# Second-level products of halves in the last projection of a cross-attention block

## The chip, the core and the metric

The program runs on one core of a Trainium2 chip. The core has TensorE (in the profile PE for its matmuls and PEld for its weight loads), VectorE (DVE), ScalarE (ACT), GpSimd (POOL) and SyncE (SP, here only a queue that issues transfers), all working side by side from their own instruction streams and waiting for one another through semaphores. Matmul results land in PSUM, eight banks of 128 x 512 float32; everything else lies in SBUF, and the large arrays in HBM. The metric is the device time of one execution in microseconds (us); smaller is better.

## The reference

Everything is float32. B = 4 batches, 512 rows of x and 512 rows of context each, D = 512, 16 heads of 32, inner width 2048.

```
x = layer_norm(hidden, ln1_w, ln1_b)
q = (x @ q_w + q_b); k = (enc @ k_w + k_b); v = (enc @ v_w + v_b)       # 16 heads of 32
attn = softmax(where(mask, q k^T / sqrt(32), min))
out = (attn v) @ cproj_w + cproj_b
hidden = out + hidden
y = layer_norm(hidden, ln2_w, ln2_b)
y = gelu(y @ fc_w + fc_b)          # "fc":   512 -> 2048
y = y @ proj_w + proj_b            # "Proj": 2048 -> 512
return hidden + y
```

## The kernel before

The whole program is one list of steps, the string ORDER. Each token names a step and its indices; the same token again carries on with that step's next part. The program emits instructions in just that order, so the string fixes the order on every engine and on every queue: an engine that must wait at its next instruction holds up all its later ones.

The front part is attention. For each of 16 groups w (4 batches by 4 groups of 4 heads) and each quarter qt of the queries: `u` makes four heads' scores on TensorE, `x` takes the maximum on VectorE and the exponentials on ScalarE, `r` transposes on VectorE, `e` exchanges blocks between partitions with 16 SBUF-to-SBUF transfers of SP's queue, `a` multiplies by v. Steps `k`, `q`, `v` make the projections, `c` the output projection. Between them lie layer norms (`s`, `r1`, `n`, `t`) and the fc step of the batch that has come through attention.

fc is made in eight chunks c per batch, each of 256 inner columns by 512 rows. A chunk is a 2 x 2 block product done by seven products of halves instead of eight (Strassen's scheme in Winograd's form): sums of weight halves by `fs` (GpSimd, function w_sums), sums of y halves by `y`, seven products in four steps `f`, then joins `j` and the gelu `g`. The result of batches 0 to 2 lies in one of two buffers of the ring `stage` until GpSimd's queue has stored it in the HBM array gd. The last batch's chunks (`lw`, `sw`, `z`, `zj`, `zg`) are made after attention, among the Proj products; there the weight sums are VectorE's, and the result stays in SBUF (`ga`).

Proj is, for each batch, again a 2 x 2 block product by seven products of halves, now of 256 columns by 256 rows by 1024 deep. `lg` loads gd into `ga`, which lies where attention's transposes were (the tile swap). `gs` makes the sums of g on VectorE (function g_sums, at most two of the three results live in the tile mix), `ps` those of the weights (p_sums, into ptt). `P` (function project, line 637 in the profile) makes one product in two halves t of 128 rows, each of 8 accumulating matmuls with a moving operand 256 wide. `J` (project_join) copies or adds the products in PSUM into the tile hids, which already holds the residual and the bias (`hd`, `pb`), and stores the rows. Four of these adds a batch run on GpSimd.

A float32 matmul of the program is two matmul records in the profile: the 448 matmuls of Proj are 896 records. Lines 281 and 284 are the helpers for one addition and one subtraction; line 278 is the helper for a transfer on SP's queue.

## Time and profile before

| what | value |
|---|---|
| median of 3 runs (lowest to highest) | 791.18 us (789.69 to 792.59) |
| profiled execution, its own time | 789.92 us |
| span of that execution, first to last instruction | 788.1 us |
| granted TensorE clock | 1.000 |
| chain that ended last, PE's share | 91% |
| attention's last scores on PE start at | 501.40 us |
| first Proj product on PE starts at | 541.29 us |
| HBM read, written | 65.03 MB, 20.97 MB |

Rows of grouped instructions read: line, engine, operation, written tile <- read tiles, shape, count | busy us, mean ns of one | idle time of the engine before them, and what ended it. Rows in order of time read: start us, length us, engine, line, operation, tiles, shape, count in a run, and in brackets the idle time before the run with its releaser. The mean of one instruction includes its latency; back to back, the next one starts before the former has ended, so rates are taken from starts.

## The change

It does three things.

Each of Proj's products is made by seven products again: its left and right factors are quartered, sums of the quarters of the left factor are made by `xs` (four VectorE operations of 512 elements for each batch and product), those of the right factor by `pt` (four, once per product number), seven sub-products with a moving operand 128 wide and 4 deep replace the two halves of 8, and `pj` joins them into a row buffer (one ScalarE copy and four VectorE adds). Three of the 28 products stay as they were (PLAIN): products 1 and 2 of batch 0 and product 4 of batch 3, which is the last of all.

The first-level sums of g are made by GpSimd as soon as a chunk has its gelu (`gs`, now per chunk: four operations of 256 elements), and stored in gd beside g by a second transfer of GpSimd's queue. gd is kept by left factor: seven blocks a batch, each loaded by one transfer of 1 MB (`la`, 28 in all, into four buffers in turn). The sums have one buffer in SBUF, 384 KB, at the end of the tile mix, where the last thirds of the second `xs` buffer and of the sums ws3 lie too.

The last batch's fc is made like the others': weight sums on GpSimd, result through `stage` and gd. All adds of `J` are VectorE's now, between SBUF operands. The bias row of Proj is loaded late (`lr`), into the place of v's. The whole list ORDER was made anew.

```diff
 ORDER = """
+k:0 k:0 wk:2 qb s1:0 s1:0 s1:0 s1:0 r1:0 n1:0 n1:0 n1:0 n1:0 k:1 t1:0:1 t1:0:1 t1:0:0 t1:0:3 t1:0:2 t1:0:0 t1:0:2 m:0
+  t1:0:3 q:0 q:0
+u:0:0 x:0:0 x:0:0 x:0:0 x:0:0 v:0 r:0:0
...
+  f:3:4 P:0:6 g:3:3 g:3:3 fs:3:5 fs:3:6 fs:3:5 fs:3:5 gs:3:3 gs:3:3 gs:3:3 gs:3:3 gs:3:3 j:3:4 j:3:4 j:3:4 j:3:4
+  fs:3:6 fs:3:5 fs:3:6 pt:6 ps:4 pt:4 pj:0:6 f:3:4 f:3:5 j:3:4 fs:3:6 g:3:4 f:3:5 f:3:5 f:3:6 P:0:5 g:3:4 j:3:5 gs:3:4
...
+  j:3:7 f:3:7 j:3:7 j:3:7 P:0:5 pj:0:6 P:0:5 J:0:1 xs:0:7 xs:0:7 P:0:7 J:0:6 xs:0:7 xs:0:3 pj:0:7 la:0:4 g:3:7 g:3:7
+  gs:3:6 gs:3:6 gs:3:6 gs:3:6 gs:3:6 P:0:3 P:0:7 xs:0:4 xs:0:4 pj:0:5 xs:0:3 xs:0:4 pj:0:5 gs:3:7 gs:3:7 gs:3:7 gs:3:7
+  gs:3:7 P:0:4 P:0:7 P:0:4 la:1:6 xs:0:5 xs:0:3 P:0:3 pj:0:3 pj:0:4 pt:5 pt:4 pj:0:4 pj:0:5 P:0:5 la:1:1 pj:0:7 pj:0:7
...
-    gd = [dram.tile([P, NP, 2, L], F32, tag=f"gd{b}", name=f"gd{b}") for b in range(LAST)]
+    gd = [dram.tile([P, 7, NP, HL], F32, tag=f"gd{b}", name=f"gd{b}") for b in range(B)]
...
+    gs = mix[:, 29 * D // 2 :].rearrange("p (s l) -> p s l", s=3)
+    xs = [mix[:, (9 + 3 * i) * D : (12 + 3 * i) * D].rearrange("p (s c l) -> p s c l", s=3, c=NP // 2) for i in range(2)]
...
+    ga = [swap[:, 2 * (i // 2), i % 2 * 4 * D : (i % 2 + 1) * 4 * D].rearrange("p (c l) -> p c l", c=NP) for i in range(4)]
...
+    ws3 = mix[:, 15 * D :].rearrange("p (c n) -> p c n", c=NP // 2)
...
+    def joins(g, names, key, own):
...
+        nc.scalar.copy(g[:, 1], q(0)[:, 0])
+        done(0)
+        yield
+        add(nc.vector, g[:, 0:4:3], q(1), g[:, 1:2].broadcast_to([P, 2, n]))
+        done(1)
+        yield
+        add(nc.vector, g[:, 1:3], q(2), g[:, 3:4].broadcast_to([P, 2, n]))
+        yield
+        add(nc.vector, g[:, 3], q(2)[:, 0], g[:, 2])
+        done(2)
+        yield
+        add(nc.vector, g[:, 1:3], q(3), g[:, 1:3])
+        done(3)
...
+    def g_sums(b, c):
+        g = S["g", b, c].rearrange("p i (j l) -> p (i j) l", j=2)
+        a11, a21, a12, a22 = (g[:, i] for i in range(4))
+        yield from a_sums(nc.gpsimd, a11, a12, a21, a22, gs[:, 0], gs[:, 1], a21, gs[:, 2])
+        yield
+        nc.gpsimd.dma_start(out=gd[b][:, :4, c], in_=g)
+        stage.done("g", b, c)
+        nc.gpsimd.dma_start(out=gd[b][:, 4:, c], in_=gs)
...
+    def load_g(b, n):
+        load(ga[TURN[b, n] % 4], gd[b][:, AT[n]])
...
+    def p_sums2(n):
+        b, t = p_terms(n)
+        return b_sums(nc.vector, *b, *t)
...
+    def g_sums2(b, n):
+        a, s = g_terms(b, n)
+        return a_sums(nc.vector, *a, *s)
 
     def project(b, n):
...
+        if (b, n) in PLAIN:
...
+        def product(o, x, y):
+            h = NP // 2
+            for c in range(h):
+                nc.tensor.matmul(o, x[:, c], y[:, c], start=(c == 0), stop=(c == h - 1))
...
+        product(bank(2, "p1")[:, 0], a11, b11)
+        yield
+        q = bank(3, "p26")
+        product(q[:, 0], a12, b21)
+        product(q[:, 1], s2, t2)
+        yield
+        q = bank(0, "p57")
+        product(q[:, 1], s3, t3)
+        product(q[:, 0], s1, t1)
+        yield
+        q = bank(1, "p34")
+        product(q[:, 0], s4, b22)
+        product(q[:, 1], a22, t4)
...
     def project_join(b, n):
...
+        def join(i, j, n):
+            o = h[i][:, :, j * HL : (j + 1) * HL]
+            add(nc.vector, o, o, of(n))
...
-        elif n == 7:
-            add(nc.vector, u3p, q, u2p)
-            yield
-            join(nc.gpsimd, 1, 1, u3p)
...
+        elif n == 7:
+            add(nc.vector, S["r", b, n], S["r", b, n], S["r", b, 6])
+            done(6)
+            yield
+            join(1, 1, n)
```

## What was predicted

> **What bounds the kernel now.** I read busy times first, then the waits of TensorE, then stretches of the span.

> ```profile
> PE 778.2 (99%) x4370; PEld 538.2 (68%) x4370; DVE 565.9 (72%) x1145; ACT 361.0 (46%) x764; POOL 188.6 (24%) x230
> ```
> ```profile
> PE acc L470 <- DMA swap<-swap: 3.1, 1, 3.1
> PE acc L708 <- POOL nhalf L697: 1.3, 1, 1.3
> PE sc L419 <- ACT pbt L398: 0.8, 1, 0.8
> PE sc L419 <- DVE mn L427: 0.8, 1, 0.8
> ```
> ```profile
> 500.00:550.00 50.00, 50.00 (x272) 34.49 (x271) 26.05 (x47) 16.39 (x27) 8.74 (x13) 1.00 0.96 313
> 550.00:600.00 50.00, 50.00 (x233) 43.93 (x232) 36.63 (x55) 2.40 (x4) 16.30 (x16) 1.00 0.36 139
> ...
> 750.00:788.10 38.10, 34.94 (x162) 30.40 (x161) 10.24 (x16) 0.00 (x0) 7.08 (x5) 1.00 0.18 59
> ```

> TensorE has matmuls running in 778.2 of 788.1 us; the four waits make 6.0 of the missing 9.9, the end 3.2. Of the stretches (length, then busy us of PE, PEld, DVE, ACT, POOL, clock, DMA share) the first two have no gap on PE at all, at full clock. So the time is the sum of TensorE's streams, and what counts is how long a stream takes and whether the others keep up.

> ```profile
> 541.29 3.62 PE L637 MATMUL acc<-pbt,swap 128*128 128x256 f32 x16
> 544.75 7.07 PE L637 MATMUL sc<-ptt,mix 128*128 128x256 f32 x32
> ...
> 9.51 3.73 PE L406 MATMUL acc<-ptt,ext 128*128 128x128 f32 x32
> 13.09 3.60 PE L384 MATMUL acc<-ext,ptt 128*128 128x512 f32 x8
> ```

> From start to start, 16 records 256 wide take 3.45 us, 0.216 each; 32 records 128 wide (v's projection, a new weight load for each) take 3.58, 0.112 each.

> **TensorE's saving.** A product was 2 x 8 matmuls, 32 records: 32 x 0.216 = 6.91 us. It becomes 7 x 4 matmuls, 56 records of v's very shape: 56 x 0.112 = 6.27. That is 0.64 less, and 25 products of 28 change: **-16.0 us**. The other bound is the mean by group, where run-outs count too:

> ```profile
> L406 PE MATMUL acc<-ptt,ext 128*128 128x128 f32 x512 | 60.8, 277 | 0.0
> ```

> 60.8 / 512 = 0.119 a record, 6.65 a product, -6.4 us in all. I take -16.0, since v's records stand in a closed stream as the new ones will. fc's matmuls are as many as before.

> **The head.** Before the first scores, v:0 (the 32 records above) filled a wait; in the new list it stands behind them.

> ```profile
> 13.60 1.91 DVE L313 TENSOR_SCALAR xn<-xn,mv,rs 128x512 f32<-128x512 f32 x4 [1.45 <-POOL rs L300]
> 16.52 2.16 PE L320 MATMUL acc<-ident,xn 128*128 128x128 f32 x16
> 22.91 1.14 PE L419 MATMUL sc<-pbt 32*128 32x512 f32 x8 [0.78 <-ACT pbt L398]
> ```

> The transposes need normalized rows, ready at 15.5. Without v:0 TensorE is free at 13.1 instead of 16.5, can transpose about 1.0 sooner, and owes 3.58 of work: **+2.6 us**. The wait of 3.1 for an exchange may go: its transfers stand a block earlier in SP's list, ahead of the four context loads that they followed. Between 0 and -3.1, I take **-1.6**.

> **VectorE's new work**, from these rows:

> ```profile
> 686.23 0.69 DVE L284 TENSOR_TENSOR mix<-mix,swap 128x512 f32<-128x512 f32 x1
> 686.83 0.69 DVE L281 TENSOR_TENSOR swap<-sc,swap 128x512 f32<-128x512 f32 x1
> ...
> L281 DVE TENSOR_TENSOR ext<-sc,ext 128x256 f32<-128x256 f32 x8 | 3.4, 421 | 20.2 <-POOL ext L281 13.5 <-PE sc L637 6.7
> ```

> An add of 512 costs 0.60 from start to start, one of 256 0.42 less the same overlap, 0.34. For 128 no row exists; the step from 512 to 256 carried on gives 0.20, and the bounds are 0 and 0.34. I split the new tail in two. **Stretch A**, from the first step of the last batch's fc to batch 1's first product: TensorE has 8 fc chunks of 28 records 256 wide, 48.3, and product steps and a transpose of 32.1, so 80.4 us. VectorE has 51 adds between two SBUF tiles (18 xs, 21 pt, 7 ps, 3 y, 2 J; 30.6), fc's joins (24 of 512, 8 of 256; 17.1) and 4 of the rest: 52. **Stretch B**, from there to the end: TensorE 20 products at 6.27, 3.5 left over from batch 0 and the plain one at 6.9, 135.8; VectorE 82 xs, 41 J, 6 pt (129 x 0.60 = 77.4), pj 67 of 256 and 22 of 128 (27.2), and 0.7: 105. So VectorE is at 65% and 78%, and its price is nothing as long as TensorE's streams cover it; if that cover goes, each us is one.

> GpSimd takes some cover away:

> ```profile
> 574.26 1.76 DVE L284 TENSOR_TENSOR ptt<-pbt,ptt 128x512 f32<-128x512 f32 x1
> 575.94 1.75 DVE L284 TENSOR_TENSOR swap<-swap 128x512 f32<-128x512 f32 x1
> 577.61 1.75 DVE L284 TENSOR_TENSOR ptt<-pbt,ptt 128x512 f32<-128x512 f32 x1
> ...
> 572.80 7.69 POOL L281 TENSOR_TENSOR ext<-ext,row 128x512 f32<-128x512 f32 x5
> ```

> ```profile
> 737.25 1.71 POOL L281 TENSOR_TENSOR ext<-ext,row 128x512 f32<-128x512 f32 x1
> ...
> L281 POOL TENSOR_TENSOR xn<-xn,row 128x512 f32<-128x512 f32 x16 | 20.4, 1274 | 135.4 <-DMA xn<-x_dram 135.3
> ...
> 686.54 2.92 POOL L281 TENSOR_TENSOR ext<-ext,row 128x512 f32<-128x512 f32 x2 [56.67 <-DMA ext<-xa]
> ```

> VectorE adds between SBUF tiles take 1.75 instead of 0.69 while GpSimd adds: 1.07 lost, and GpSimd's own go from 1.27 to 1.71. The add from PSUM of the row 686.83 stays at 0.69, although GpSimd was adding then. Stretch B has 12 bias adds on GpSimd: 12 x 1.07 = 13, so VectorE needs 118 of 135.8. The slack is thin, xs, pj and J share one queue, and a J that waits for a bias holds up the xs behind it. Bounds 0 and +8; I take **+2**.

> [...]

> **GpSimd's chain in stretch A** is the dearest doubt.

> ```profile
> 485.92 0.74 POOL L281 TENSOR_TENSOR wsum<-ext 128x256 f32<-128x256 f32 x1
> 486.74 0.74 POOL L284 TENSOR_TENSOR ext<-ext 128x256 f32<-128x256 f32 x1
> 487.43 0.73 POOL L284 TENSOR_TENSOR wsum<-wsum,ext 128x256 f32<-128x256 f32 x1
> ...
> L578 POOL DMA_DIRECT2D gd<-st x24: 531/571/622, 204.5 to 558.5; - x24
> ...
> DMA to landing us min/median/max: 2.9/5.0/7.5
> ```

> The sums of g have one buffer, so a chunk's first sum waits until the former chunk's store has landed. A cycle is four sums at 0.70, 0.57 for the issue of g, then 5.0 from the issue of the sums to their landing: 8.4 us; the weight sums (fs, 2.8) and bias adds lie inside that wait. From the first chunk's last step to the eighth's TensorE has 41.4 us of fc and 8.1 of product steps between: 7.1 per chunk. So GpSimd falls 1.3 behind per chunk, 9 after seven. Who waits: product 5 of batch 0 needs its last xs sum, which is written where this buffer lies; in TensorE's list 14.4 us of steps stand between the last fc step and that one, and the last joins, gelu, sums and landing take about 1.3 + 1.4 + 2.8 + 5.6 + 0.7 = 11.8. The stall is 9 - 2.6 = 6.4; with landing at 3.5 us there is none. The stores now go in runs of 1 KB (512 pieces instead of 128), which no row shows: an issue costs between 0.57 and, at four times, 2.3. With 2.3 for each of the two, and GpSimd's sums stretched in collisions by 0.45 (1.27 to 1.71), a cycle takes up to 11 and the stall reaches +25. Nearest are the rows of stores of the same kind in a chip less loaded than in attention (DMA share 0.36 against 0.96): I take **+5**, range 0 to +25.

> In attention the sums of 24 chunks bring 24 x 3.4 = 82 us to a GpSimd that is busy for 188.6 in the whole span, most chunks a score block or more from the next; VectorE there works mostly with one SBUF operand, which no row shows disturbed. I take 0. The loads and the end:

> ```profile
> swap<-gd SPq DMA_DIRECT2D x12, 1024.0 KB, 8.1
> ```
> ```profile
> 777.87 7.07 PE L637 MATMUL sc<-ptt,swap 128*128 128x256 f32 x32
> 784.98 0.42 DVE L281 TENSOR_TENSOR ext<-sc,ext 128x256 f32<-128x256 f32 x1 [2.96 <-PE sc L637]
> ```

> The 28 loads of 1 MB, 8.1 us from issue to landing, have four buffers and 6.3 us per product, so three products (19 us) cover one: 0 as well. The last half product, its add and its store keep their form, and the 3.2 us after the last matmul stay.

> **Sum.** 789.9 - 16.0 + 2.6 - 1.6 + 5 + 2 = **781.9 us**. The profiled run's 789.92 is 1.3 below the median of the runs, 791.18; I leave the forecast at 782.

> **Rivals.**
> 1. *All of it is covered.* No stall in A or B, the exchange wait gone: 789.9 - 16.0 + 2.6 - 3.1 = 773.4. For it: VectorE's 65% and 78%. Against: the 8.4 us cycle.
> 2. *GpSimd becomes the bound of the last fc, slower.* Place: the one buffer of sums and the stage ring. It decides once the cycle exceeds 9.9: then lag 7 x 2.8 less 2.6 is 17, all that the rest of the sum (776.9) leaves to 793.6. At 12.2 us (landing at 7.0, collisions 1.8) the stall is 33: 810. For it: landings up to 7.5, four times the pieces. Against: median 5.0 under heavier traffic.
> 3. *VectorE becomes the bound of stretch B.* It decides when a product costs VectorE over 6.8 us; it now costs 105 / 20 + 0.65 = 5.9. If each of the 20 products waits 1 us in its queue, time is 782 + 20 - 2 = 800. For it: 220 adds in one list. Against: no engine of the old tail shows such waits on PE.
> 4. *The narrow streams don't gain what a closed stream gains*, 0.119 a record: 781.9 + 9.6 = 791.5, no change.

> **How the numbers follow.** Chances: forecast (776 to 788) 0.50, rival 1 0.18, rival 2 0.17, rival 3 0.10, rival 4 0.05. Below 772 or above 800 lies most of rival 2's upper half and little else, about 0.15. What a measurement can tell from no change is about 0.3%, 788.8 to 793.6: faster 0.50 + 0.18 + 0.03 of rival 3 = 0.71; slower 0.17 + 0.06 = 0.23; the same 0.06.

> **What would show it.** Rows of `P` 128 wide at 0.112 from start to start and PE busy near 762 confirm the saving. The head is right if PE idles about 2.5 us ahead of the first transposes. [...] It is wrong if PE busy doesn't fall by some 16, or if PE's waits exceed 25 us.

## The result, and the profile after

The changed kernel takes 831.38 us (829.35 to 834.29) where the kernel before, in four runs now, takes 790.45 (789.69 to 792.59): 1.0516 times as long, 95% interval 1.0476 to 1.0556. The forecast was 782, the range ended at 800. The profiled execution took 832.2 us, 50.3 more than the 781.9 of the sum.

The busy times of the page of after, and TensorE's longest waits there (for whom: total us, times, longest):

```profile
PE 779.2 (94%) x4970; PEld 553.4 (67%) x4970; DVE 651.4 (78%) x1290; ACT 371.0 (45%) x791; POOL 326.1 (39%) x414
```
```profile
PE acc L565 <- ACT st L589: 10.7, 6, 5.4
PE acc L565 <- POOL wsum L321: 5.9, 2, 4.5
PE acc L702 <- DVE mix L321: 5.8, 2, 5.2
PE acc L507 <- issue: 4.6, 1, 4.6
PE sc L702 <- DVE st L318: 3.5, 2, 2.7
```

Line 565 is fc's product, 702 the second-level product, 507 the step that multiplies by v; 589 is ScalarE's first copy of a chunk into a stage buffer, 318 and 321 are the helpers for one addition and one subtraction. Span less busy time is 51.2 us. The forecast had 17.9 idle (9.9 + 2.6 - 1.6 + 5 + 2) and 762.2 busy, so 33.3 us are more idle time and 17.0 are matmuls that ran longer.

Stretches of after (length, then busy us of PE, PEld, DVE, ACT, POOL, clock, DMA share, GB/s):

```profile
500.00:550.00 50.00, 43.56 (x252) 29.30 (x250) 31.77 (x62) 25.05 (x44) 34.26 (x48) 1.00 0.82 231
...
600.00:650.00 50.00, 41.35 (x211) 35.44 (x210) 37.72 (x44) 10.19 (x19) 44.66 (x55) 0.93 0.42 145
650.00:700.00 50.00, 41.43 (x314) 40.27 (x313) 34.70 (x63) 2.67 (x7) 11.52 (x14) 0.90 0.49 173
700.00:750.00 50.00, 50.00 (x450) 50.00 (x449) 44.67 (x80) 2.19 (x9) 8.88 (x6) 1.00 0.65 212
```

Before, PE was busy throughout 500 to 600. Now 6 to 9 us are lost in each of the first three stretches shown. In the last fc (600 to 650) GpSimd, 39% busy over the span, is busy for 44.7 of 50 us, and the clock is below 1. Where Proj alone runs (700 to 750) there is no gap, and the narrow products go at the forecast rate, 8 records in 0.89 us:

```profile
705.04 1.06 PE L702 MATMUL acc<-pbt,swap 128*128 128x128 f32 x8
705.94 1.06 PE L702 MATMUL sc<-ptt,mix 128*128 128x128 f32 x8
706.83 1.06 PE L702 MATMUL sc<-mix,swap 128*128 128x128 f32 x8
```

How a wait comes about, from the rows of GpSimd and then of PE at the end of attention (start, length; in brackets the idle time before, and its releaser):

```profile
467.24 0.75 POOL L622 DMA_DIRECT2D gd<-mix  x1
...
475.43 0.72 POOL L318 TENSOR_TENSOR mix<-st 128x256 f32<-128x256 f32 x1 [5.99 <-DMA gd<-mix]
476.23 0.73 POOL L321 TENSOR_TENSOR st<-st 128x256 f32<-128x256 f32 x1
476.92 0.73 POOL L321 TENSOR_TENSOR mix<-mix,st 128x256 f32<-128x256 f32 x1
477.60 0.73 POOL L321 TENSOR_TENSOR wsum<-pbt,wsum 128x256 f32<-128x256 f32 x1
```
```profile
478.38 2.08 PE L565 MATMUL acc<-yT,wsum 128*128 128x256 f32 x4 [4.52 <-POOL wsum L321]
```

The next chunk's first sum waits 5.99 us for the former store to land. A weight sum for another chunk stands three instructions behind it, and TensorE stands still until that is made. At the place that the prediction named, product 5 of batch 0, rows of GpSimd, VectorE and PE in three fences:

```profile
599.67 0.79 POOL L620 DMA_DIRECT2D gd<-st  x1
...
668.45 1.17 POOL L321 TENSOR_TENSOR mix<-mix,st 128x256 f32<-128x256 f32 x1
669.70 1.06 POOL L321 TENSOR_TENSOR mix<-st,mix 128x256 f32<-128x256 f32 x1
670.70 0.79 POOL L620 DMA_DIRECT2D gd<-st  x1
671.49 0.75 POOL L622 DMA_DIRECT2D gd<-mix  x1
```
```profile
676.03 0.69 DVE L321 TENSOR_TENSOR mix<-swap,mix 128x512 f32<-128x512 f32 x1 [5.52 <-issue]
```
```profile
677.50 2.08 PE L702 MATMUL acc<-swap,mix 128*128 128x128 f32 x8 [5.22 <-DVE mix L321]
```

The store of the last batch's first chunk is issued at 599.67 and that of its last at 670.70, seven cycles of 10.1 us. The last sums leave at 671.49, VectorE's sum that is written over them starts at 676.03, and PE waits 5.22. (The last two stores of sums land 3.9 and 4.4 us after their issue starts.) Its 8 records then take 2.08 us instead of 1.06, since the clock fell meanwhile (stretches of 1 us):

```profile
674.00:675.00 1.00, 0.00 (x0) 0.00 (x0) 0.00 (x0) 0.00 (x0) 0.00 (x0) 1.00 1.04 422
...
676.00:677.00 1.00, 0.00 (x0) 0.00 (x0) 0.94 (x2) 0.00 (x0) 0.00 (x0) 0.50 0.00 0
...
681.00:682.00 1.00, 1.00 (x7) 1.00 (x6) 0.04 (x1) 0.00 (x0) 0.00 (x0) 0.50 0.00 0
...
683.00:684.00 1.00, 1.00 (x11) 1.00 (x11) 1.00 (x3) 0.00 (x0) 0.00 (x0) 1.00 0.48 66
```

Some 3.5 us into the gap the granted clock is halved, and it stays so for about 5 us of work: 2.6 us lost on top of the gap. Summed over stretches of 0.5 us, seven gaps of 2.2 to 5.4 us cost 12.9 us of clock in this way, most of the 17.0.

## The experiments

The theories tested first were S (the one buffer of sums), R (the ring of two stage buffers) and Q (GpSimd's work itself). Each table row gives the median of the runs of that kernel, its ratio to the kernel before run beside it with the 95% interval, and, from its one profiled execution: the start of the last batch's first fc step on PE, the time from there to the end of its last fc step, and from there to the end of the last matmul.

| kernel | us | ratio | first fc step | last fc | behind it |
|---|---|---|---|---|---|
| after | 831.38 | 1.0516 (1.0476 to 1.0556) | 579.7 | 73.5 | 173.7 |
| neither sums nor second store | 782.37 | 0.9936 (0.9856 to 1.0016) | 559.3 | 62.0 | 155.8 |
| sums alone | 799.55 | 1.0146 (1.0077 to 1.0216) | 563.6 | 74.0 | 158.5 |
| second store alone | 798.79 | 1.0135 (1.0092 to 1.0178) | 573.6 | 62.1 | 156.1 |
| second store alone, by SP | 793.29 | 1.0042 (1.0004 to 1.0081) | 569.6 | 61.9 | 156.2 |
| sums of 16 columns alone | 783.86 | 0.9932 (0.9899 to 0.9964) | 560.2 | 62.6 | 155.7 |
| those with a fill behind each | 815.11 | 1.0302 (1.0190 to 1.0414) | 580.4 | 70.3 | 160.0 |
| both for batches 0 to 2 | 809.25 | 1.0228 (1.0050 to 1.0405) | 580.8 | 62.5 | 155.9 |
| both for batch 3 | 805.01 | 1.0174 (1.0059 to 1.0290) | 558.5 | 70.2 | 169.3 |
| two buffers of sums | 817.66 | 1.0353 (1.0249 to 1.0457) | 581.6 | 69.2 | 158.9 |
| three stage buffers | 834.33 | 1.0564 (1.0462 to 1.0666) | 585.5 | 73.1 | 167.8 |
| both rings larger | 817.42 | 1.0373 (1.0281 to 1.0465) | 584.4 | 73.6 | 156.8 |
| two buffers, weight sums first | 814.18 | 1.0298 (1.0188 to 1.0408) | 576.5 | 71.0 | 161.4 |
| batch 3's sums on VectorE | 841.54 | 1.0679 (1.0635 to 1.0724) | 583.0 | 80.8 | 172.0 |
| batch 3's weight sums on VectorE | 828.35 | 1.0464 (1.0424 to 1.0504) | 581.8 | 76.5 | 164.7 |
| that with two buffers | 813.41 | 1.0275 (1.0218 to 1.0332) | 574.0 | 75.6 | 157.0 |
| that for batch 2 too | 820.09 | 1.0360 (1.0299 to 1.0420) | 580.2 | 76.7 | 156.4 |
| all products plain | 823.67 | 1.0418 (1.0287 to 1.0549) | 581.4 | 75.8 | 158.8 |

How well such marks repeat: up to the last fc, "both for batch 3" is the kernel with neither, and "both for batches 0 to 2" is after. Their rows of the first step, and those of neither and of after:

```profile
558.51 1.17 PE L565 MATMUL acc<-yT,ext 128*128 128x256 f32 x4
```
```profile
559.28 1.17 PE L565 MATMUL acc<-yT,ext 128*128 128x256 f32 x4
```
```profile
580.76 1.17 PE L565 MATMUL acc<-yT,ext 128*128 128x256 f32 x4
```
```profile
579.70 1.17 PE L565 MATMUL acc<-yT,ext 128*128 128x256 f32 x4
```

These agree within about 1 us. Another pair, two buffers of sums with and without batch 3's weight sums on VectorE, has group 15's first scores at 479.9 and 483.2, ahead of any difference between the two kernels. So differences of the marks below 4 us are not read.

**The rings.**

```diff
-    gs = mix[:, 29 * D // 2 :].rearrange("p (s l) -> p s l", s=3)
+    gs2 = const.tile([P, 3 * HL], F32, tag="gs2", name="gs2")
+    gs_of = [t.rearrange("p (s l) -> p s l", s=3) for t in (mix[:, 29 * D // 2 :], gs2)]
...
-    stage = Ring(const.tile([P, 2 * L], F32, tag=f"st{i}", name=f"st{i}") for i in range(2))
+    stage = Ring(const.tile([P, 2 * L], F32, tag=f"st{i}", name=f"st{i}") for i in range(3))
```

> The changed kernel with two buffers of 3 KB per partition for GpSimd's sums of g, used in turn, instead of one. The room comes from the bias rows: one row serves all three biases, so the biases added are not the reference's; the instructions are the same. Theory S (one buffer of sums: GpSimd stands 33.1 us in 11 waits for gd<-mix to land, its later weight sums stand behind that, and TensorE behind those): these waits go to under 5 us, PE's idle time from 45.7 to about 20, the granted clock rises to about 0.99 and the time falls to 795 to 805. Theory R (the ring of two stage buffers holds ScalarE's first copy of a chunk, 45.1 us in 17 waits): the stage waits stay, 820 to 830. Theory Q (GpSimd has simply too much in its queue next to each chunk): 820 to 830 too.

> The changed kernel with three stage buffers instead of two; the sums keep their one buffer. The room comes from the bias rows as in the run before (one row for all three biases, so the biases are not the reference's) and from fewer buffers for the small tiles of the layer norms. Theory R: ScalarE's waits for gd<-st fall from 45.1 to under 10 us, PE's waits on the copy into st (10.7 + 3.1 us, and what the clock loses after them) go, 800 to 810. Theory S: a chunk still waits at its sums, 820 to 830, with GpSimd's waits for gd<-mix at 30 us or more. Theory Q: 820 to 830.

> The changed kernel with both two buffers for GpSimd's sums and three stage buffers. The room comes from one bias row for all three biases, from t4 of y lying in t1's place and s4 of fc's weights in s1's place, so the biases and two of fc's seven products are not the reference's; the instructions are as many. Theory: once the sums' landing no longer holds GpSimd's queue, the stage ring is what is late next (37.1 us of ScalarE's waits, 10.6 us of PE's with two buffers of sums alone): 796 to 806, PE idle near 22 us. If a third stage buffer is worth nothing here either, as it was alone, 812 to 818.

Two buffers take 14 us off, fewer than theory S gave and more than R and Q did. By the marks they gain 14.8 behind the last fc, where product 5's last sum needn't wait for the last landing any more, 4 in it, and nothing ahead of it: the wait of 5.99 us shown above isn't what attention loses by. A third stage buffer is worth nothing, alone (834, above all bands) or with the second buffer of sums: theory R falls. With both rings larger the stretch from 600 to 650 reads:

```profile
600.00:650.00 50.00, 40.19 (x195) 34.50 (x194) 36.71 (x46) 8.40 (x17) 47.11 (x57) 0.97 0.44 149
```

GpSimd is busy for 47.1 of 50 us. With little left to wait for in this stretch it is close to being a bound itself.

**Sums and store, one by one.** Four kernels make a square: both, either, neither.

```diff
-        yield from a_sums(nc.gpsimd, a11, a12, a21, a22, gs[:, 0], gs[:, 1], a21, gs[:, 2])
+        for _ in range(4):
+            yield
...
-        nc.gpsimd.dma_start(out=gd[b][:, 4:, c], in_=gs)
```

> The changed kernel without GpSimd's four sums per chunk (128 instructions, 102 us of its busy time): both stores stay, the second one stores zeros, so products 3, 5, 6 and 7 of Proj are not the reference's. Theory Q: PE idle falls below 15 us and the time to 780 to 790. Theory S: the landing wait is now one for the issue of the next store alone, most of it gone as well, 790 to 800. Theory R: stores are issued about 3 us sooner, so half of the stage waits go, 805 to 815. If the second-level products or their sums on VectorE are what costs, the time stays above 820.

> The changed kernel without the second store of each chunk: GpSimd still makes the four sums, but nothing of them goes to gd, and products 5, 6 and 3 of Proj load g's own first three blocks instead, 1 MB each as before, so these products are not the reference's. It takes away the landing that the one buffer of sums waits for, 24 us of issues on GpSimd and 12.6 MB of traffic. If the landing is the whole matter, it equals the run with two buffers, 812 to 818; if GpSimd's issues and the traffic count too, 800 to 808; if GpSimd's adding time is what counts, it stays above 818, since the run without sums gave 799.

> The changed kernel with neither GpSimd's sums nor the second store (products 3, 5, 6 and 7 of Proj are not the reference's). What is left of the change is the new order, the second-level products and the last batch's fc made through the stage buffers. If the second-level products give what they were forecast to give, 779 to 785, with PE idle near 14 us. If the second store's traffic and issues don't matter, it equals the run without the sums, 796 to 801; if the second-level products themselves lose, above 790 as well, with waits of PE inside Proj.

Neither: 782.4, where the forecast's sum without its 5 us for GpSimd gives 776.9. Busy times of that kernel, and its stretches of the last fc and of Proj:

```profile
PE 762.5 (98%) x4970; PEld 543.8 (70%) x4970; DVE 637.8 (82%) x1290; ACT 370.8 (48%) x791; POOL 202.9 (26%) x254
```
```profile
600.00:650.00 50.00, 48.88 (x375) 46.85 (x374) 41.96 (x78) 7.34 (x16) 7.89 (x9) 1.00 0.36 124
650.00:700.00 50.00, 50.00 (x450) 50.00 (x450) 46.45 (x85) 2.20 (x9) 9.14 (x6) 1.00 0.70 240
700.00:750.00 50.00, 49.93 (x444) 49.55 (x444) 38.10 (x72) 1.76 (x7) 5.89 (x4) 1.00 0.65 228
```

TensorE is busy for 762.5 us, and Proj runs without gaps. So the second-level products and the loads lose nothing there; the 5 us more are idle time (18.1 of the span against 12.9), short waits in attention. Even this kernel is not told apart from the one before (0.9936, up to 1.0016). The sums alone cost 17 us, the store alone 16, both 49. The marks show where. Ahead of the last fc the store costs 14.3 and the sums 4.3 (both: 20.4). In the last fc the sums cost 12 and the store nothing. Behind it only the two together cost anything, 17.9.

**What of the store costs.** The second store of zeros, from SP's queue:

```diff
-        nc.gpsimd.dma_start(out=gd[b][:, 4:, c], in_=gs)
+        nc.sync.dma_start(out=gd[b][:, 4:, c], in_=gs)
```

> As the run without GpSimd's sums (799 us), but the second store, of zeros, is issued by SP's queue instead of GpSimd's; products 3, 5, 6 and 7 of Proj are not the reference's. The bytes and pieces are the same, and GpSimd is spared 32 issues. Leaving this store out altogether took the time from 799 to 782. If GpSimd's 24 us of issues are what it costs, 782 to 787. If it is the traffic (12.6 MB more among the exchanges of attention), 794 to 801, with PE's waits for the exchanges as they were.

793.3, just under the band given for the traffic: of the 16 us about 5 go with GpSimd's issues and 11 stay, all ahead of the last fc. That these are the bytes is not shown, though, because SP's queue also issues attention's loads, and the stores hold it up. One of TensorE's two longest waits in attention, 3.23 us, is for a load of fc's weights. Rows of SP with neither sums nor store, then of SP and PE with the store by SP:

```profile
464.46 0.91 SPq L315 DMA_DIRECT2D pbt<-fc_w_dram  x2
```
```profile
458.91 1.98 SPq L622 DMA_DIRECT2D gd<-mix  x3
...
467.50 1.01 SPq L315 DMA_DIRECT2D pbt<-fc_w_dram  x2
```
```profile
474.55 2.05 PE L565 MATMUL acc<-yT,pbt 128*128 128x256 f32 x4 [3.23 <-DMA pbt<-fc_w_dram]
```

Three stores take 2.0 us of the queue, the loads behind them are slower to issue, and this one is issued 3.0 us later. Nor are the pieces the same: the stores are 12,800 packets from SP's queue and 3,584 from GpSimd's. So the price of the bytes by themselves stays open; the exchanges' median time to landing, 3.0 us, is the same with neither and with GpSimd's store alone.

**What of the sums costs.**

```diff
+        a11, a12, a21, a22, s1, s2, s4 = (a[:, :16] for a in (a11, a12, a21, a22, *(gs[:, i] for i in range(3))))
...
+            nc.gpsimd.memset(mix[:, 29 * D // 2 : 29 * D // 2 + 720], 0.0)
```

(The second added line, once behind each of the four sums, is that of the run with the fill.)

> As the run without the second store (799.6 us), but each of GpSimd's sums covers 16 columns instead of 256: as many instructions at the same places with the same waits, a small part of the adding time. Products 3, 5, 6 and 7 of Proj are not the reference's. If the 17 us that the sums cost there come from the time they take on GpSimd (0.76 to 0.86 each) and from VectorE's loss beside them, 782 to 788. If they come from the place of the waits (a sum that waits for the gelu holds the weight sums behind it), 794 to 801.

> As the run with sums of 16 columns and no second store (783.9 us), with a fill of 720 columns of the sums' buffer on GpSimd behind each of the short sums, so that GpSimd is about as long at work as with the full sums but writes only and reads nothing. Products 3, 5, 6 and 7 of Proj are not the reference's. If the 17 us of the full sums (799.6 us) are GpSimd's own time in its queue, 795 to 802. If they are what VectorE and GpSimd take from one another when both work on SBUF (VectorE was busy 652.5 us with the full sums, 636.3 with the short ones), 782 to 788 and VectorE's busy time stays near 637, unless a fill disturbs it as an add does.

The short sums cost 1.5 us, so the place of the waits costs nothing by itself. Busy times with full sums, with short ones, and with short ones and the fill:

```profile
PE 767.6 (96%) x4970; PEld 545.3 (68%) x4970; DVE 652.5 (82%) x1290; ACT 370.6 (46%) x791; POOL 300.6 (38%) x382
```
```profile
PE 764.9 (98%) x4970; PEld 544.3 (70%) x4970; DVE 636.3 (81%) x1290; ACT 370.6 (47%) x791; POOL 232.7 (30%) x382
```
```profile
PE 772.9 (95%) x4970; PEld 547.1 (67%) x4970; DVE 637.5 (78%) x1290; ACT 370.9 (46%) x791; POOL 321.3 (39%) x510
```

With the fill GpSimd is busy 21 us longer than with the full sums, VectorE is undisturbed (637.5), and the time is 815, worse than the band. GpSimd's time alone is enough to do harm. The 16 us that VectorE loses beside full sums (652.5 against 636.3) aren't needed for it; that they cost nothing isn't shown. In the last fc the fill costs 8 us where the full sums cost 12, but ahead of it 21 where they cost 4, so it does not stand for the sums there; why stays open.

**Attention and the last fc.**

```diff
-        nc.gpsimd.dma_start(out=gd[b][:, 4:, c], in_=gs)
+        if b < LAST:
+            nc.gpsimd.dma_start(out=gd[b][:, 4:, c], in_=gs)
```

(The sums go by the same condition; the other run has `b == LAST`.)

> The changed kernel with sums of g and second stores for batches 0 to 2 only, which lie in attention; the last batch's are left out (its products 3, 5, 6 and 7 are not the reference's). With neither anywhere it was 782.4, with both everywhere 831.4. In the traces of these two, the last batch's first fc step on PE starts 20 us apart, so 800 to 806 if the attention part is a cost by itself; 785 to 790 if what attention loses is given back in the tail.

> The changed kernel with sums of g and second stores for the last batch only; those of batches 0 to 2 are left out (their products 3, 5, 6 and 7 are not the reference's). From the last batch's first fc step to the end, the trace with both everywhere is 29 us longer than the one with neither. If that is the cost of the last fc's sums by themselves, 807 to 815; if the stretch is only long because GpSimd enters it late from attention, 788 to 798.

+27 and +23 to neither, 50 together where both cost 49. Both times lie outside their bands, and the two runs of the first are 9 us apart. By the marks, from one execution each, batches 0 to 2 cost 21.5 us ahead of the last fc and nothing from there; batch 3 costs 21.7 from there, where after loses 29.4. So what attention loses is not given back, and by these marks some 8 us of the rest come only with both.

**Order and place of GpSimd's work.** Weight sums ahead of the sums of g that stood between them, with two buffers of sums (52 tokens of ORDER moved, the first place of them here):

```diff
-  fs:0:4 fs:0:4 fs:0:4 gs:0:2 gs:0:2 gs:0:2 gs:0:2 fs:0:4 gs:0:2
+  fs:0:4 fs:0:4 fs:0:4 fs:0:4 gs:0:2 gs:0:2 gs:0:2 gs:0:2 gs:0:2
```

> The kernel with two buffers of sums (817.7 us; one bias row for all three biases, so these are not the reference's), with 52 of GpSimd's weight sums moved ahead of the sums of g that the order put between them and their chunk's first weight sum. Nothing but GpSimd's order changes. If fc's weight sums are late because they stand behind sums of g that wait for their gelu, PE's waits in fc's steps (8.9 us of 33.9) and part of the clock's loss go: 800 to 808. If GpSimd's time itself is short, the sums of g come later by as much, ScalarE waits longer for a stage buffer, and the time stays at 812 to 820.

814.2 against 817.7: not told apart from no gain. Then the last batch's sums of g, and in other runs its weight sums, on VectorE:

```diff
+        yield from a_sums(nc.vector if b == LAST else nc.gpsimd, a11, a12, a21, a22, gs[:, 0], gs[:, 1], a21, gs[:, 2])
```
```diff
+        "fs": lambda b, c: w_sums(nc.vector if b == LAST else nc.gpsimd, b, c)
```

> The changed kernel with the last batch's sums of g (32 of the 128) on VectorE instead of GpSimd; its output is the reference's. If the stretch of the last fc is held by GpSimd's cycle, PE's gaps there (17 us between 600 and 680, and some 6 us that the clock loses after them) go, against about 12 us of VectorE work that has room there: 805 to 815. If VectorE's own queue is the holder there (xs, pt and the joins behind one another), the gaps stay or grow: 828 to 845.

> The changed kernel with the last batch's 32 weight sums of fc on VectorE, where the kernel before had them; GpSimd keeps all sums of g. Its output is the reference's. If GpSimd's own time per chunk is the bound of the last fc (3.0 of weight sums, 3.4 of sums of g, 1.55 of two issues, so 8 us against the 7.1 that TensorE has), it falls to 5 us there, TensorE waits for landings only, and the time is 812 to 820. If VectorE's own queue is the bound of that stretch, its 11 us more make it 835 to 845.

> The same with two buffers of sums (one bias row for all three biases, so these are not the reference's). With GpSimd's time and the landing both out of the last fc, its 23 us go but for VectorE's share of 2 to 6: 798 to 806. If it stays at 812 to 818, as two buffers alone gave, the last fc has another bound.

> As the last, with batch 2's weight sums on VectorE too (one bias row for all three biases). Batch 2's fc stands at the end of attention, where GpSimd was busy 34.3 of the 50 us from 500 to 550 and VectorE 31.8. If GpSimd's time is also what the end of attention waits for, 788 to 798; if it is the traffic of the second store, as the store issued by SP's queue (793 against 782) says for some 11 us, it stays at 798 to 806.

The sums of g on VectorE are 10 us slower than on GpSimd: the second answer given, a queue in which a wait for a gelu or a landing holds up joins and xs. The weight sums on VectorE gain 3 us (outside both bands) and, with two buffers, 4 (in the second), where 11 to 19 were expected from GpSimd's time as the one bound; batch 2's cost 7 more, outside both bands. With two buffers and GpSimd relieved, PE's and ScalarE's longest waits from 570 to 670 are

```profile
PE acc L566 <- ACT st L590: 8.7, 3, 6.1
```
```profile
ACT st L613 <- DVE st L319: 37.8, 7, 9.6
ACT st L590 <- DMA gd<-st: 16.2, 5, 5.7
```

TensorE now waits for the copy into a stage buffer, which waits for a store to land and, before that, for joins that stand late in VectorE's queue. So the last fc has at least two limits of nearly one length: GpSimd's time (47.1 of 50 busy with larger rings), and the way round the stage ring when GpSimd is relieved. Taking off one at a time gains little. Both at once, a third stage buffer beside VectorE's weight sums, wasn't tried. Theory S holds behind the last fc, theory Q for one of the limits in it; attention loses mostly by the store, in a way that is open.

**Plain products.**

```diff
-PLAIN = ((0, 1), (0, 2), LATE)
+PLAIN = tuple(TURN)
```

> All 28 products plain as in the earlier run of that kind, but each product's two halves stand together in the order, ahead of the copy that reads them; the output is the reference's. GpSimd's sums and both stores stay. If the second-level products lose nothing of their 16 us, the sums of g cost here what they cost with them, 49 us, and the time is about 845. If the second-level work of VectorE is what makes GpSimd's chain late in the last fc, the gaps after 600 us are gone and the time is 818 to 828, as in the earlier run (823.9).

823.7, in the second band. (In the earlier run that this text names, ScalarE's copy of a product stood before the product's second half, so its output was not the reference's.) So with GpSimd's sums in place the narrow products make the kernel about 8 us slower instead of 16 faster. From the last batch's first fc step to the last matmul, plain products take 234.6 us: within 1 us what the kernel with neither takes (217.8) and the 16.0 that narrow products save. After 600 us PE has one gap over 0.25 us, of 1.92. So with plain products the sums and stores cost nothing there, and after's 29 us in this stretch are a cost of the two parts of the change together. There is no xs to be written over the sums' buffer and no product that waits for it, VectorE has less to do, and TensorE's longer list fills the 10.2 us from store to store that GpSimd takes here too; which of these counts most was not tried.

No version that makes the whole computation came below the kernel before.

## Why the prediction was wrong, step by step

**TensorE's -16.0: right.** 762.5 busy without sums and store, 762.2 forecast. In after it is 779.2: 12.9 of the 17.0 are the clock's loss behind gaps, a term that the prediction did not have; the other 4.1 I haven't divided. (The other bound of the term is -6.5 by its own figures, not -6.4.)

**The head, +2.6: right.** The first scores of after:

```profile
21.91 1.14 PE L456 MATMUL sc<-pbt 32*128 32x512 f32 x8 [0.78 <-ACT pbt L435]
```

1.00 sooner than before's 22.91, with 3.58 of v:0 still to do. **The exchange wait, -1.6:** the wait of 3.1 is gone, so it came to the far end of its range, -3.1.

**VectorE in stretch B, +2:** 0 without sums and store (no gap from 650 to 750); one wait of 2.9 in after. **Loads, 0: right**, no wait of PE on them in the kernel with neither.

**GpSimd in attention, "I take 0": the step that failed.** It cost 20 us up to the last fc. The working weighed 82 us of sums against 188.6 us of busy time in the whole span, an average. Its 3.4 us a chunk are four sums at 0.70 and, as it seems, one issue at 0.57; what the second store's 9.4 MB do among transfers that were 0.96 busy, and what its issue does to the work behind it, had no price. The store was the greater part: 14.3 alone, 10.3 even when SP issued it, against 4.3 for the sums alone. Whether by its bytes or by its place in a queue stays open.

**Stretch A, +5: the place right, the size wrong.** It cost 29: 12 in the last fc and 18 behind it. The step that failed is "the weight sums and bias adds lie inside that wait", which gave a cycle of 8.4 us and a lag of 9. The rows of after:

```profile
L321 POOL TENSOR_TENSOR mix<-mix,st 128x256 f32<-128x256 f32 x32 | 27.5, 859 | 0.1
L321 POOL TENSOR_TENSOR mix<-st,mix 128x256 f32<-128x256 f32 x32 | 25.8, 806 | 1.9
L620 POOL DMA_DIRECT2D gd<-st x32 | 25.3, 790 | 0.0
L321 POOL TENSOR_TENSOR st<-st 128x256 f32<-128x256 f32 x32 | 24.6, 770 | 2.1
L318 POOL TENSOR_TENSOR mix<-st 128x256 f32<-128x256 f32 x32 | 24.5, 764 | 158.1 <-ACT st L612 94.5 <-DMA gd<-mix 33.1 <-DVE st L318 15.2
L622 POOL DMA_DIRECT2D gd<-mix x32 | 24.1, 752 | 0.0
```

Sums 3.2, two issues 1.54 and the weight sums, 2.8 in the prediction, make 7.5 us of GpSimd's own time per chunk, with no wait at all and without the bias adds, against the 7.1 that TensorE has. From the first of the last fc's stores shown above to the last, seven cycles of 10.1 us, GpSimd is busy for 54.8 of 71.0 us, 7.8 a cycle. It waits for a landing for 7.6 in all, and once for 7.2 us for a join of VectorE. So GpSimd's own work is most of the cycle, and the landing, which made it in the forecast, is little of it. The 18 us behind the last fc are the forecast place, product 5's sum over the one buffer (two buffers take 15 of them away), with a lag of 21 us (seven times 10.1 less 7.1) where 9 were forecast, about half of it lost in the last fc already, and the clock's loss on top. The upper bound was too low by its own terms: four sums at 1.15, an issue of 2.3 and a landing of 5.0 make a cycle of 11.9, not 11, and a stall of 31, not 25.

**The rivals.** The second, GpSimd as the bound of the last fc through its ring of sums and the stage ring, came nearest, with its place and its sign. Its 810 is the last fc's part alone (805 measured for batch 3's sums and stores); it lacked attention. Its condition, a cycle over 9.9, was met: 10.1 from store to store. The first, third and fourth rivals did not occur.

**The issue of 512 pieces**, bounded by 0.57 and 2.3, took 0.79. **The collisions** came in after's last chunk: GpSimd's four sums there (666.41 to 670.76) took 0.95 to 1.17 instead of 0.73, and three of VectorE's adds between SBUF tiles beside them 0.88 to 1.21 instead of 0.69. The fill, which writes but reads nothing, left VectorE's busy time as it was (637.5 against 636.3). It did the harm all the same.

## What to carry to other kernels

Before work is moved to an engine that looks idle, add up its own instructions per iteration in the tightest stretch, DMA issues included, and only then the waits; a share of the whole span says nothing there. A new store has a price even where nobody waits for it, 16 us here: count its issues in the queue that makes them and its bytes among the transfers of that stretch. Add what the clock loses to a gap on TensorE: here seven gaps of 2.2 to 5.4 us cost 12.9 us of slower clock behind them, some 2 us each, and one of 2.77 cost none.

## What the runs showed of the hardware

```profile
354.18 2.21 PE L443 MATMUL acc<-ptt,ext 128*128 128x128 f32 x12 [2.22 <-DVE mn L464]
...
519.71 1.50 PE L507 MATMUL acc<-swap,mix 128*32 128x256 f32 x24 [2.77 <-ACT st L589]
```
```profile
355.00:356.00 1.00, 1.00 (x7) 1.00 (x7) 1.00 (x3) 0.22 (x2) 0.00 (x0) 0.50 1.05 263
...
521.00:522.00 1.00, 1.00 (x15) 0.44 (x10) 1.00 (x4) 1.00 (x3) 0.42 (x1) 1.00 0.92 274
```

The shorter gap halved the clock for some 3.4 us, the longer one didn't. The slow stretches ahead of after's last matmul are 3.41 us long (five) or 6.83 (two), and they start whole multiples of 3.41 us apart. On that grid TensorE was idle for 65% of the 3.41 us that end where the clock falls behind the gap of 2.22 (351.52 to 354.94), but for only 54% and 27% of the two pieces over which the gap of 2.77 is spread (515.36 to 518.78, and on to 522.19). In the trace of after, each of the 8 pieces of this grid at full clock with 65% idle or more was followed by a slow one; of the 225 with 54% or less, none was. The gap of 2.22 us lies within one piece, that of 2.77 in two; why the clock falls is not shown. One issue of a store by GpSimd takes 0.79 us for 512 pieces and 0.75 for 384 (means of 32 in after), against 0.57 for 128 (median of 24 in before).
